# A two-layer graph network on one core: the first layer without the edges of nodes to themselves

## The chip, the core and the metric

The kernel runs on one core of a Trainium2 chip, in one launch. The metric is the time of the launch on the device in microseconds (us). The profile records one further execution of the same kernel, instruction by instruction.

## The reference, cut to what matters

There are 6250 nodes with 512 float32 features each, and 106250 directed edges: 50000 random ones, the same ones reversed, and one edge of each node to itself. They arrive sorted by destination (`dst`), and stably, so that a node's own edge is the last edge of its list (the own edges were appended last).

```python
def layer0(x, src, dst):                      # weights W_l, b_l, W_r
    agg = segment_sum((x @ W_l.T + b_l)[src], dst)     # sum over incoming edges
    deg = segment_sum(1, dst)
    return agg / max(deg, 1) + x @ W_r.T
x = layernorm(x + layer0(x, src, dst))

def layer1(h, src, dst):                      # summed by src: edges have to be sorted anew
    neigh = segment_sum((h @ W_neigh.T + b_neigh)[dst], src) / max(deg, 1)
    y = h + relu(h @ W_self.T + b_self + neigh)
    return layernorm(y) * ln_gamma + ln_beta
x = layernorm(x + layer1(x, src, dst))
```

## The kernel before, in words

**Tiles, runs and groups.** Both layers are done by `grouped` (L640 on). The sorted edges lie in tiles of 128 edges. For every tile, GpSimd (POOL) issues one indirect DMA that gathers the 128 source rows (2 KB each, 256 KB in all) into a row buffer; that is `fetched`, L633. There are 40 row buffers, used in turn. The edges are further cut into *runs* (the code calls them windows): stretches of edges whose nodes, at most H = 32, are summed together. In layer 0 a run is 3.5 tiles (CYCLE 2, 7: two runs every seven tiles), in layer 1, which leaves out the own edges, 3.25 tiles (CYCLE_L 4, 13). The nodes are divided into C = 4 parts, and one *group* takes one run of each part, so 4 x 32 rows of output. Layer 0 has 238 runs in 60 groups, layer 1 has 241 in 61.

**One group.** `match` (L180, `hot<-rel,cols`) builds on VectorE (DVE), for each tile of a run, a 128 x 32 matrix of zeros and ones: which edge belongs to which of the 32 nodes. `visits` (L740) multiplies that matrix with the gathered rows and adds up in PSUM (`agg`). The four runs of a group use four 32-column strips of TensorE (PE) side by side; I call the four matmuls that visit one tile of each run a *round*. A round is 8 records in the trace, since every float32 matmul has two. Runs of layer 0 touch 5 or 4 tiles in turn, because a run that ends within a tile shares that tile with the next one. `count` (L749) counts edges per node, `average` (L771) divides on ScalarE (ACT), `turn` transposes (L612, L614), `dense` projects by the two weight matrices (L620), `close` and `store` add bias and own rows, normalize (L554 to L570) and write the group's rows, 32 per part, to DRAM: `h_d` after layer 0, the output after layer 1. A group's own rows are loaded by SP (L727), 4 transfers per group, at a row number that SP reads from `lo_i`; the last groups, which would reach beyond the table, use an indirect DMA on POOL for it (L722), and for their stores as well (L793).

**Order of the work.** The order is written out by hand (`manual_schedule`), engine by engine. In the loop over groups g: `fetch(g+1)`, `match(g+1)`, the first two rounds of g, the transposed mean and the own projection of g-1, `store(g-2)`, `begin(g+1)` (own rows), the third round, the mean projection of g-1, own transpose, the other rounds, `count` and `average` of g, `close(g-1)`, then up to one step of the "other work" that uses PE, `shrink(g+1)` (L679), and up to five steps that use DVE alone. The other work in layer 0 is the sort of the edges by `src` for layer 1, a bitonic sort on DVE with transposes on PE (`Sorter.runs`). Layer 1 can start only when all of `h_d` is written.

**Start.** `first_rows` loads the indices of group 0, so that 19 gathers can start at once. `as_given` loads the edge lists (`given_k`, `next_i`, `given_v`), turns them by transposes into one column per tile (`node`, `idx`), `place` works out where runs begin and end (`lo`, `rel`) and whether the data fit this scheme (`flag`). If the flag is not zero, a slow fallback (`plain`, one tile after another) does the layer instead.

The lines that the prediction speaks of: L633 row gathers, L740 aggregation, L749 counting, L612 and L614 transposes, L620 projections, L180 the helper `both` (hot, sort steps, sums), L271 to L279 the first operations of the sort (`Sorter.load`), L722 and L793 indirect loads and stores of the last groups, L727 and L800 own rows and stores by SP.

Of the kernel before, what the change touches and what calls it, by code (L numbers as in the profile page):

```python
# [21 lines left out]
CYCLE = 2, 7  # L22
CYCLE_L = 4, 13
# [75 lines left out]
def kernel(  # L99
# [116 lines left out]
    class Sorter:  # L216


        def __init__(self, key, val, layer, pool, ps, loops, given=None):

            self.given = given
            self.pool, self.ps, self.layer, self.loops = pool, ps, layer, loops
            self.M = M if not loops else (E - N + P - 1) // P
            n, T = self.cycle = CYCLE_L if loops else CYCLE
            self.NW = (n * self.M + T - 1) // T

            Q = self.Q = (self.NW + C - 1) // C


            starts = [i * T * P // n - 1 for i in range(n + 1)]
            self.at = [v // P for v in starts[:n]]
            self.row_at = [v % P for v in starts[:n]]
            self.num = [b // P - a // P + 1 for a, b in zip(starts, starts[1:])]
            self.vis = max(self.num)
            self.key, self.val = key, val
            self.cur = None
            self.padded = const.tile([P, 1 + W], F32, name=f"node{layer}")
            self.node = self.padded[:, 1:]  # L240
            self.idx = const.tile([P, W], I32, name=f"idx{layer}")
            self.lo = const.tile([P, C * Q + 1], F32, name=f"lo{layer}")
            self.lo_i = const.tile([1, C * Q + 1], I32, name=f"lo_i{layer}")
            self.X = 1 if loops else 0
            self.rel = const.tile([P, Q, self.X + self.vis, C], F32, name=f"rel{layer}")
            self.flag = const.tile([1, 1], I32, name=f"flag{layer}")
            if loops:

                a = (E - N - CAP - 1) // P
                self.row = pool.tile([P, M - a], F32, name="row")  # L250
                nc.gpsimd.iota(self.row, pattern=[[P, M - a]], base=a * P - (E - N) + LOOP,
                               channel_multiplier=1, allow_small_or_imprecise_dtypes=True)
                self.more = const.tile([P, 1], F32, name="more")
                self.parts = 2 + (M - a - 1) // (W // CAP // 2 * 2)
# [10 lines left out]
        def load(self):  # L265
# [3 lines left out]
            if self.loops:  # L269
                v = self.pool.tile([P, W], I32, name="next_i")  # L270
# [76 lines left out]
        def as_given(self):  # L347


            full = M - 1  # L350
            ints = []
            for i, (v, fill, skip, eng) in enumerate((
                (self.key, NONE, 0, nc.sync), (self.key, NONE, 1, nc.scalar),
                (self.val, NONE, 0, nc.sync),
            )):
                t = self.pool.tile([P, blocks, P], I32, name=("given_k", "next_i", "given_v")[i])
                nc.vector.memset(t[:, full // P:, :], fill)
                a = full // P
                if a:
                    eng.dma_start(t[:, :a, :], v[skip:skip + a * P * P]  # L360
                                  .rearrange("(b p c) -> p b c", p=P, c=P))
                b = full % P
                if b:
                    eng.dma_start(t[:b, a, :], v[skip + a * P * P:skip + full * P]
                                  .rearrange("(p c) -> p c", c=P))
                r = E - full * P - skip
                if r:
                    eng.dma_start(t[b:b + 1, a, :r], v[skip + full * P:E].unsqueeze(0))
                ints.append(t)
            key, nxt, val = ints  # L370
            self.given = [t.rearrange("p b c -> p (b c)") for t in (key, val)]

            def columns(t, o):
                f = self.pool.tile([P, blocks, P], F32, name="srt", bufs=2)
                nc.vector.tensor_copy(f, t)
                p = self.ps.tile([P, 2 * D], F32, name="turn")
                for b in range(blocks):
                    nc.tensor.transpose(p[:, b * P:(b + 1) * P], f[:, b, :], ident)
                nc.scalar.copy(o[:, :D], p[:, :D])
                if o is self.idx:  # L380
                    nc.vector.tensor_scalar(o[:, D:W], p[:, D:W], float(N - 1), None, op0=ALU.min)
                else:
                    nc.vector.tensor_copy(o[:, D:W], p[:, D:W])

            columns(key, self.node)
            nc.vector.tensor_tensor(nxt, key, nxt, op=ALU.is_gt)
            worst = self.pool.tile([P, 1], F32, name="worst")
            nc.vector.tensor_reduce(worst, nxt.rearrange("p b c -> p (b c)"),
                                    axis=mybir.AxisListType.X, op=ALU.max)
            p = self.ps.tile([P, 2 * D], F32, name="turn")  # L390
            nc.tensor.matmul(p[:1, :1], worst, ones[:, :1], start=True, stop=True)
            odd = self.pool.tile([1, 2], F32, name="mixed")
            nc.vector.memset(odd, 0.0)
            nc.vector.tensor_copy(odd[:, :1], p[:1, :1])
            self.odd = odd
            return lambda: columns(val, self.idx)

        def first_rows(self):

            self.first = const.tile([P, C, self.vis], I32, name="first")  # L400
            for c in range(C):
                t = self.tiles(c * self.Q)
                k = max(0, -t.start)
                v = self.val[(t.start + k) * P:t.stop * P]
                nc.scalar.dma_start(self.first[:, c, k:len(t)], v.rearrange("(t p) -> p t", p=P))

        def unpack(self):
# [3 lines left out]
            n = self.pool.tile([P, W], I32, name="next_i")  # L411
# [69 lines left out]
        def place(self):  # L481
# [47 lines left out]
            if Q % n:  # L529
                nc.vector.memset(self.rel, -1.0)  # L530
# [11 lines left out]
            if self.loops:  # L542
                nc.vector.tensor_scalar(
                    self.rel[:, :, 0, :], lo[:, :C * Q].rearrange("p (c q) -> p q c", c=C), -1.0,
                    self.more, op0=ALU.mult, op1=ALU.add)
# [22 lines left out]
    def finish0(nr, po, own, some, work):  # L568
        po = po[:nr]
        nc.vector.scalar_tensor_tensor(po, biases["bl"][:nr], some[:nr], po,  # L570
                                       op0=ALU.mult, op1=ALU.add)
# [51 lines left out]
    def fetched(s, table, g, chunks, idx):  # L623


        for v in range(0 if g == 0 else 1, s.vis):
            for c in range(C):
                w = c * s.Q + g
                m = s.tiles(w)[v:v + 1]
                if w < s.NW and m and 0 <= m[0] < s.M:  # L630
# [5 lines left out]
                if w < s.NW and v == 1 and g:  # L636
                    t = s.tiles(w - 1)
                    chunks[w, 0] = chunks[w - 1, len(t) - 1]

    def grouped(s, table, w_n, w_s, layer, finish, dest, other, chunks, loads):  # L640
# [3 lines left out]
        with tc.tile_pool(name=f"g{layer}", bufs=2) as work, tc.tile_pool(  # L644
# [14 lines left out]
            def fetch(g):  # L659
                fetched(s, table, g, chunks, s.idx)  # L660
# [347 lines left out]
```

## Time and profile before

| what | us |
| --- | --- |
| median of 3 runs (2104.13 to 2106.35) | 2106.04 |
| the profiled execution | 2107.11 |
| its span, first to last instruction | 2105.3 |
| PE busy in the span | 1942.8 (92%) |
| POOL busy | 1558.7 (74%) |
| DVE busy | 1156.5 (55%) |
| first row gather issued | 5.94 |
| last row gather of layer 0, first of layer 1 | 1066.97, 1091.55 |
| last row gather of layer 1 | 2074.6 |

The profile's rows are to be read so. In the list in order of time, a row gives start, duration, engine, line, operation, output <- input, shape, how many were merged (`x8`), and in brackets how long the engine had been idle before and what ended that. In the list of groups, a row gives busy time and the mean in ns of one, then the idle time in front of them. A time of PE is not PE at its peak: a matmul that waits for its operands in the pipe counts as busy. `issue` stands for idle time in which the engine waited for nothing that the profile shows.

### The profile page before, as it was taken

Reading aid. Unit: us, or ns where it says so; the run is one execution under the profiler, and the core shown is the slowest. Engines: PE = TensorE matmul, PEld = TensorE weight load, DVE = VectorE, ACT = ScalarE, POOL = GpSimd, SP = SyncE. Lnnn points to the kernel's source line nnn. Section 1 sums busy time; section 2 is a strip of 40 time slices with the busy share of each in tenths; the row PEclk is TensorE's granted clock in tenths of the full one; section 3 lists DMA queues with packets and bytes.
Section 4 is the critical chain, followed back from the end, with each engine's and each line's share of the span. In section 5 each row is a group of like instructions: output and inputs, shape, how many; then the busy total and the mean of one; then the engine's idle time right before and its main releaser. Section 6 shows DMA issues by size and latency. Waiting matters only on the chain.

```text
span 2105.3 us, 26581 instructions
## 1 busy us (share of the span) xinstructions
PE 1942.8 (92%) x7561; PEld 658.8 (31%) x7561; DVE 1156.5 (55%) x2417; ACT 302.4 (14%) x631; POOL 1558.7 (74%) x1638
## 2 busy tenths in 40 slices
PE   4899999999999999999879999999999999999996
PEld 2333333333333333332322333333333333333332
DVE  4754455645555554342434556665666566655676
ACT  0111111111111111111101111111111111111111
POOL 7777777777777777777747777777777777777773
PEclk9999999999999999999989999999999999999998
DMA  9777778787888887878757788888878888887874
GB/s 265 223 231 234 239 235 239 238 240 237 244 253 251 252 247 239 238 235 241 230 149 220 240 245 244 241 240 243 247 241 240 244 244 244 240 240 244 245 240 122
DMA packets 184969, 495.94 MB, mean 236 GB/s; under 512 B 45911, under 2 KB 48401, under 8 KB 184806
## 3 DMA queue, kind: packets, MB, share of 16 engines
q0 software_dynamic: 130128, 426.15, 68.2%
q1 hardware_dynamic: 48308, 61.99, 9.4%
q10 hardware_dynamic: 6370, 5.94, 0.9%
q8 instruction: 64, 1.05, 0.2%
q14 instruction: 99, 0.81, 0.1%
HBM read 462.59 MB, written 31.65 MB: 235 GB/s over the span
## 4 chain that ended last, share of the span: by engine, by line
PE 55%; DMA 30%; issue 7%; POOL 6%; DVE 2%; POOLq 0%; ACT 0%; SPq 0%; ACTq 0%; DVEq 0%
PE po L620 29%; PE agg L740 20%; DMA rows<-h_d,idx 16%; DMA rows<-in_x_dram,idx 14%; POOL rows L633 6%; PE tp L612 4%; PE turn L308 0%; PE deg L749 0%; PE turn L469 0%; DMA first<-in_src_dram 0%; DMA own<-in_x_dram,slots 0%; DVE stats L554 0%; DVE po L570 0%; DVE v L180 0%; DVE srt L180 0%
## 5 line engine op out<-in xcount | busy, mean ns | idle before, releaser
L740 PE MATMUL agg<-rows,hot 128*32 128x512 f32 x4180 | 939.4, 614 | 105.4 <-DMA rows<-h_d,idx 41.0
L633 POOL DMA_INDIRECT rows<-in_x_dram,idx x815 | 786.7, 965 | 248.0 <-issue 116.8
L633 POOL DMA_INDIRECT rows<-h_d,idx x785 | 743.9, 948 | 241.6 <-issue 113.0
L620 PE MATMUL po<-wa,meanT 128*128 128x512 f32 (+1 forms) x968 | 447.5, 605 | 0.0
L620 PE MATMUL po<-wb,ownT 128*128 128x512 f32 (+1 forms) x968 | 436.3, 593 | 0.1
L740 PEld LDWEIGHTS agg<-rows,hot 128*32 128x32 f32 x4180 | 163.7, 109 | 667.0 <-DMA rows<-in_x_dram,idx 229.4
L603 DVE TENSOR_SCALAR inv<-deg 128x1 f32<-128x1 f32 (+1 forms) x60 | 9.5, 158 | 488.8 <-PE deg L749 488.8
L620 PEld LDWEIGHTS po<-wa,meanT 128*128 128x128 f32 (+1 forms) x968 | 173.0, 188 | 275.3 <-issue 254.4
L620 PEld LDWEIGHTS po<-wb,ownT 128*128 128x128 f32 (+1 forms) x968 | 173.8, 190 | 175.2 <-issue 174.9
L758 DVE TENSOR_SCALAR loops<-deg 128x1 f32<-128x1 f32 (+1 forms) x61 | 9.6, 158 | 341.1 <-PE deg L749 341.0
L180 DVE SCALAR_TENSOR_TENSOR srt<-srt 128x448 f32<-128x448 f32 (+3 forms) x313 | 180.4, 618 | 4.0
L614 ACT COPY ownT<-tp 128x512 f32<-128x512 f32 (+1 forms) x121 | 70.3, 581 | 758.9 <-PE tp L612 758.9
L679 DVE TENSOR_REDUCE hotb<-hot 128x128 bf16<-128x640 f32 x121 | 142.0, 1173 | 0.1
L771 ACT ACTIVATE mean<-agg,inv 128x512 f32<-128x512 f32 (+1 forms) x121 | 83.1, 687 | 386.7 <-DVE agg L767 177.3
L558 ACT ACTIVATE rstd<-mv,eps 128x1 f32<-128x1 f32 (+1 forms) x182 | 53.6, 295 | 415.5 <-DVE mv L556 410.6
L180 DVE SCALAR_TENSOR_TENSOR hot<-rel,cols 128x768 f32<-128x768 f32 (+1 forms) x121 | 102.3, 846 | 0.0
L614 ACT COPY meanT<-tp 128x512 f32<-128x512 f32 (+1 forms) x121 | 70.2, 580 | 204.1 <-PE tp L612 204.1
L612 PEld LDWEIGHTS tp<-ident,own 128*128 128x128 f32 (+1 forms) x484 | 60.5, 142 | 76.9 <-issue 74.2
L612 PEld LDWEIGHTS tp<-ident,mean 128*128 128x128 f32 (+1 forms) x484 | 51.1, 142 | 106.2 <-issue 53.5
L612 PE MATMUL tp<-ident,own 128*128 128x128 f32 (+1 forms) x484 | 73.1, 274 | 12.1 <-DMA own<-in_x_dram,slots 6.7
L612 PE MATMUL tp<-ident,mean 128*128 128x128 f32 (+1 forms) x484 | 79.6, 287 | 3.6 <-ACT mean L771 3.6
L564 DVE TENSOR_SCALAR po<-po,mv,rstd 128x512 f32<-128x512 f32 (+1 forms) x61 | 50.0, 819 | 2.2
(147 smaller groups left out, 879.0 us busy)
## 6 DMA issues: line engine op xcount, KB each, us to landing
own<-h_d SPq DMA_DIRECT2D x241, 64.0 KB
own<-in_x_dram SPq DMA_DIRECT2D x230, 64.0 KB
out_dram<-y SPq DMA_DIRECT2D x230, 64.0 KB
h_d<-y SPq DMA_DIRECT2D x227, 64.0 KB
rows<-in_x_dram,idx POOLq DMA_INDIRECT x815
rows<-h_d,idx POOLq DMA_INDIRECT x785
wa<-in_L_gnn_W_l_dram ACTq DMA_DIRECT2D x4, 256.0 KB
wb<-in_L_gnn_W_r_dram ACTq DMA_DIRECT2D x4, 256.0 KB
```

The lines of the kernel that those rows point to most:

```text
L180: nc.vector.scalar_tensor_tensor(o, a, 1.0, b, op0=ALU.mult, op1=op)
L558: nc.scalar.activation(root[:nr], mv[:nr, 1:2], AF.Sqrt, bias=eps[:nr])
L564: nc.vector.tensor_scalar(y, v, mv[:nr, 0:1], root[:nr], op0=ALU.subtract, op1=ALU.mult)
L603: nc.vector.tensor_scalar(inv[:nr], deg, 1.0, None, op0=ALU.max)
L612: nc.tensor.transpose(p[:, k, :nr], v[:nr, k * P:(k + 1) * P], ident[:nr, :nr])
L614: nc.scalar.copy(t[:, :, :nr], p[:, :, :nr])
L620: nc.tensor.matmul(po[:nr], aT[:, k, :nr], w[:, k, :], start=first and k == 0, stop=end and k == NK - 1)
L633: nc.gpsimd.indirect_dma_start(out=rows, out_offset=None, in_=table, in_offset=bass.IndirectOffsetOnAxis(ap=at, axis=0))
L679: nc.vector.tensor_reduce(hb[:, 0, :], hots[g][:, s.X * C:n * C].rearrange("p (v c) h -> p (c h) v", c=C), axis=mybir.AxisListType.X, op=A ...
L740: nc.tensor.matmul(agg[H * c:H * (c + 1), :], hot[:, C * (s.X + v) + c, :], chunks[w, v], start=v == have[0], stop=v == have[-1])
L758: nc.vector.tensor_scalar(st["loops"][:nr], deg[:nr, 1:2], 1.0, None, op0=ALU.add)
L771: nc.scalar.mul(st["mean"][:nr], st["agg"][:nr], st["inv"][:nr])
```

## The change

Layer 0 gets its own class, `Given`, beside `Sorter`, which from now on serves layer 1 alone.

- Runs of layer 0 are now 3 whole tiles long (`TILES = 3`), plus the last tile of the run before: 4 rounds per group throughout. There are 66 runs per part, 264 in all, so 66 groups. In each part the first 4 runs (`WIDE`) hold 384 edges as given. The other 62 are cut from the list every 404 edges (`RAW`); their own edges are taken out, and what remains (384 if 20 were taken, less if more were) fits the same 3 tiles. The sum for such runs gets its own rows added (`average`), and 1 is added to the count (`count`).
- Taking them out happens on the chip. 124 partitions hold two runs each; every edge knows how many places it has to move (0 to 31, from the count of nodes before it), and five rounds of "shift those with bit i by 2^i" pack them (`narrow`). These operations are the first pieces of the other work in the loop, ahead of the sort: all of the DVE ones stand behind `shrink(1)` of group 0, the transposes (`turned`) and the copies into `idx`, `node` and `rel` (`placed`) in group 1.
- Because the packed indices are not there at the start, the indices of groups 0 to 3 are loaded separately: `first` for group 0 and `lines`, turned by a transpose into `second`, for groups 1 to 3. The gathers of group 1 are issued ahead of the flag as well (`EARLY = 2`).
- Where runs begin is no longer found by matmuls but loaded from `dst` (`li`, `back`), so that SP's row numbers come from DRAM directly. The test of the data (`flag`) checks the numbers of nodes per run among others.
- The 40 row buffers become a ring of fixed tiles. `finish0` adds the bias without the factor `some`.

The built program issues 795 row gathers in layer 0 where 834 stood, and 47 transfers on SP and ACT ahead of the weights of layer 0 where 13 stood; on POOL, one of the two own-row gathers of the last groups now stands behind the last row gather.

The diff, cut to its core:

```diff
-CYCLE = 2, 7
-CYCLE_L = 4, 13
+CYCLE = 4, 13
+TILES = 3
+WIDE = 4
+RAW = 404
+FEWEST = RAW - TILES * P
+MOST = 31
+EARLY = 2
 ROWS = 40
...
+    class Given(Sorter):
+        loops = False
+        def shape(self):
+            self.X, self.vis, self.M = 0, TILES + 1, M
+            self.wide = WIDE * TILES * P
+            part = (E + C - 1) // C
+            self.pairs = (part - self.wide + 2 * RAW - 1) // (2 * RAW)
+            self.Q = WIDE + 2 * self.pairs
+            self.NW = C * self.Q
...
+        def rows(self, w, v):
+            c, g = divmod(w, self.Q)
+            m = TILES * g + v
+            if g == 0:
+                return self.first[:, c, v:v + 1]
+            if g < WIDE:
+                return self.second[:, c * self.near_cols + m:c * self.near_cols + m + 1]
+            return self.idx[:, c * self.cols + m:c * self.cols + m + 1]
...
+        def ask(self, spare):
...
+            for t, k, d, eng in ((self.li, 2, -1, nc.scalar), (self.back, 1, -1 - BACK, nc.sync)):
+                for c in range(C):
+                    for g, step, num in ((0, TILES * P, WIDE), (WIDE, RAW, self.Q - WIDE)):
...
+                        eng.dma_start(
+                            t[:, w:w + num - skip, :],
+                            bass.AP(tensor=dst.tensor, offset=dst.offset + at,
+                                    ap=[[E, 1], [step, num - skip], [1, k]]))
...
+            for t, v, fill in ((self.wk, dst, N), (self.wv, src, 0)):
...
+                    nc.sync.dma_start(
+                        t[c * pairs:c * pairs + k, :],
+                        bass.AP(tensor=v.tensor, offset=v.offset + c * L + self.wide,
+                                ap=[[2 * RAW, k], [1, 2 * RAW + 1]]))
...
+        def turn_lines(self):
+            n = 2 * C * self.near_cols
+            f = self.fresh()
+            nc.vector.tensor_copy(f[:n, :P], self.lines[:n])
+            p = self.ps.tile([P, 2 * D], F32, name="turn")
+            nc.tensor.transpose(p[:, :n], f[:n, :P], ident[:n, :n])
...
+        def narrow(self):
...
+            def taken():
+                two(a, w, val, ALU.is_equal)
+                two(b, w, nxt, ALU.not_equal)
+                two(a, a, b, ALU.bitwise_and)
+            def moves():
+                by_bits(a, a, -1, ALU.add)
+                two(pairs(b), pairs(w), pairs(w)[:, :, :1].to_broadcast([top, 2, RAW]),
+                    ALU.subtract)
+                by_bits(b, b, 2 * BITS, ALU.logical_shift_left)
+            def packed():
+                nc.vector.tensor_scalar(w, w, NONE, BITS, op0=ALU.bitwise_xor,
+                                        op1=ALU.logical_shift_left)
+                two(w, w, val, ALU.bitwise_or)
+                two(w, w, b, ALU.bitwise_or)
+                two(w, w, a, ALU.bitwise_and)
+            def move(i):
+                d = 1 << i
+                nc.vector.tensor_scalar(b, w, 31 - 2 * BITS - i, 31, op0=ALU.logical_shift_left,
+                                        op1=ALU.arith_shift_right)
+                two(b, b, w, ALU.bitwise_and)
+                two(w, w, b, ALU.bitwise_xor)
+                to = pairs(w)[:, :, :RAW - d]
+                two(to, to, pairs(b)[:, :, d:], ALU.bitwise_or)
...
+            def turned():
+                p = self.ps.tile([P, 2 * D], F32, name="turn")
+                f = pairs(self.wk[:top, :n].bitcast(F32))
+                for j in range(2 * TILES):
+                    i, m = divmod(j, TILES)
+                    nc.tensor.transpose(p[:, j * P:j * P + top], f[:, i, m * P:(m + 1) * P],
+                                        ident[:top, :top])
+                self.x = self.fresh()
+                nc.scalar.copy(chunks(self.x), chunks(p))
+            def placed():
...
+                nc.vector.tensor_scalar(u, x, BITS, NONE, op0=ALU.logical_shift_right,
+                                        op1=ALU.bitwise_and)
...
+                for c in range(C):
+                    nc.vector.tensor_scalar(to[0][:, c], of[0][:, c], NONE, None,
+                                            op0=ALU.bitwise_and)
+                    nc.vector.tensor_scalar(to[1][:, c], of[1][:, c], -1.0, float(NONE),
+                                            op0=ALU.mult, op1=ALU.add)
+                self.nodes_less_first(self.node, m, WIDE, self.Q)
+            runs = [taken, moves, packed, *(lambda i=i: move(i) for i in range(5)), end]
+            for i in range(0, len(runs), 2):
+                yield False, lambda i=i: [r() for r in runs[i:i + 2]]
+            yield True, turned
+            yield False, placed
...
                 if not s.loops:
-                    st["inv"], st["some"] = inverse(deg[:nr, :1], nr, work)
+                    st["inv"] = work.tile([P, 1], F32, name="inv")
+                    nc.vector.tensor_scalar(st["inv"][:nr], deg[:nr, :1], 1.0, None,
+                                            op0=ALU.max if g < WIDE else ALU.add)
+                    nc.vector.reciprocal(st["inv"][:nr], st["inv"][:nr])
                     return
...
+                elif g >= WIDE:
+                    both(st["agg"][:nr], st["agg"][:nr], st["own"][:nr], ALU.add)
                 st["mean"] = work.tile([P, D], F32, name="mean")
...
-    s0.first_rows()
+    s0.ask((s1.padded.bitcast(I32), s1.idx))
+    s1.given, s1.next = s0.given[::-1], s0.next
     first = {}
-    fetched(s0, x, 0, first, s0.first)
-    rest = s0.as_given()
+    fetched(s0, x, 0, first)
+    s0.turn_lines()
+    for g in range(1, EARLY):
+        fetched(s0, x, g, first)
...
+    def meanwhile():
+        yield from s0.narrow()
+        yield from sort_and_place(s1)
...
-        grouped(s0, x, *w0, 0, finish0, h_d, sort_and_place(s1), first, loads)
+        grouped(s0, x, *w0, 0, finish0, h_d, meanwhile(), first, loads)
```

In the original, `a` and `b` are scratch tiles of 124 x 808 int32, `w` and `val` the destinations and sources of two runs per partition, `nxt` the destinations one place further on, `two` a tensor_tensor and `by_bits` a tensor_scalar on DVE.

## The prediction

> **What bounds the kernel now.** I read the engine totals first, then one steady stretch of POOL and PE in order of time, then the longest waits, then the start and the seam between the layers. The totals and the group of row gathers:
>
> ```profile
> PE 1942.8 (92%) x7561; PEld 658.8 (31%) x7561; DVE 1156.5 (55%) x2417; ACT 302.4 (14%) x631; POOL 1558.7 (74%) x1638
> ...
> L633 POOL DMA_INDIRECT rows<-in_x_dram,idx x815 | 786.7, 965 | 248.0 <-issue 116.8
> L633 POOL DMA_INDIRECT rows<-h_d,idx x785 | 743.9, 948 | 241.6 <-issue 113.0
> ```
>
> PE looks like the bound at 92%. The order of time contradicts it, POOL first, then PE in the same stretch:
>
> ```profile
> 412.01 0.95 POOL L633 DMA_INDIRECT rows<-in_x_dram,idx  x1 [0.30 <-PE agg L740]
> 413.26 0.95 POOL L633 DMA_INDIRECT rows<-in_x_dram,idx  x1 [0.30 <-DMA rows<-in_x_dram,idx]
> 414.51 0.95 POOL L633 DMA_INDIRECT rows<-in_x_dram,idx  x1 [0.30 <-PE agg L740]
> 415.76 0.95 POOL L633 DMA_INDIRECT rows<-in_x_dram,idx  x1 [0.30 <-issue]
> ```
>
> ```profile
> 414.16 0.66 PE L612 MATMUL tp<-ident,mean 128*128 128x128 f32 x4
> 414.65 3.60 PE L620 MATMUL po<-wb,ownT 128*128 128x512 f32 x8
> 418.18 1.07 PE L740 MATMUL agg<-rows,hot 128*32 128x512 f32 x8
> 419.18 3.70 PE L620 MATMUL po<-wa,meanT 128*128 128x512 f32 x8
> 422.71 0.60 PE L612 MATMUL tp<-ident,own 128*128 128x128 f32 x4
> 423.25 1.90 PE L740 MATMUL agg<-rows,hot 128*32 128x512 f32 x10
> 426.28 2.74 PE L740 MATMUL agg<-rows,hot 128*32 128x512 f32 x6 [1.14 <-DMA rows<-in_x_dram,idx]
> 428.96 0.18 PE L749 MATMUL deg<-ones_b,hotb 128*128 128x1 bf16 x1
> 429.07 4.29 PE L740 MATMUL agg<-rows,hot 128*32 128x512 f32 x16
> ```
>
> POOL starts a gather every 1.25 us (0.95 busy, 0.30 between), whatever is named as releaser, and never waits longer. PE's aggregation stretches instead: 16 records take 4.29 us where rows are late, 8 take 1.07 where they are there. So the gathers' beat sets the pace. It adds up: layer 0 has 19 + 815 row gathers and 2 of own rows, from 5.94 to 1066.97 us; 835 intervals of 1.25 are 1043.8, the rest 17.3. Layer 1 has 785, 1091.55 to 2074.6: 784 x 1.25 = 980.0, rest 3. The seam takes 24.6, the end 30.7.
>
> The Trainium skill's page "Perfetto Trace Analysis", section Identifying the Most-Contended Engine, holds occupancy to be a fair measure for GpSimd and a bad one for matmuls. The second half agrees with the 4.29 against 1.07 above; by the first half POOL at 74% would have a quarter to spare, and dropping gathers would pay only 0.95 us each (40 x 0.95 = 38 us). The rows show the 0.30 to recur like work, so the beat decides.
>
> **What the change removes.** The program as built has 795 row gathers in layer 0 (264 runs of 3 tiles, and 3 more) for 834. With one own-row gather instead of two ahead of the last row gather (the other comes behind it), intervals go from 835 to 795: **-40 x 1.25 = -50.0 us**, if the beat stays the limit. Layer 1 keeps its 785.
>
> **Does PE stay below the beat?** A new group has 12 gathers: 15.0 us. PE per group from the rows above: projections 3.60 + 3.70, transposes 0.66 + 0.60, counting 0.18, and 4 rounds of aggregation (for 5 or 4) at 1.07: 13.0 us. Groups of 12 gathers exist already: every second one in layer 0, counted from one L749 row to the next, takes about 15.2 us. The 6 added groups (66 for 60) bring PE 6 x 8.74 = 52.4 us less 6 rounds x 1.07, +46 us, inside the 2 us per group that PE has free. If that cover goes, the +46 shows: rival 1. The added sum of own rows to agg (L767's kind in layer 1: 0.76) lies between count and mean; layer 1 has the same chain and holds the beat. DVE is busy 55%, 9.6 us of the mean 17.5 per group, sort steps included, and so has room in 15. SP issues 8 transfers per group at 0.70 to 0.87 us: up to 7 of 15. The bytes per group fall slower than its time: 14 x 256 KB in 15 us is 245 GB/s, and the profile's slices of layer 1 show 240 to 247.
>
> **The start: a wait is added.** The first 51 gathers (groups 0 to 3) need no packed indices; the 52nd needs the first copy of the packing. By the beat it is due at 5.9 + 51 x 1.25 + 0.4 (flag) = 70 us. What leads to its index:
>
> 1. Loads. 47 transfers on SP and ACT, where 13 stood, and in the program as built each waits for the one eight before it. A small one needs 4.4 us here (the index list `first`, 1.27 to 5.66). So four per queue in 4.4 us, 1.1 us apart: the 18 that SP issues from 4.7 us to the last `back` end at about 22, landed by 25. Then some 8 us of short DVE rows (0.15 to 0.6 each; nbad's reduction 0.64): the first `hot` at about 33, for 28.41.
> 2. Group 0's own rows and count follow as before (inv at 43.38), so at 48. Behind it on DVE: shrink, then the packing, all 31 operations in one go.
> 3. The packing. Its operations are new; the nearest rows are these:
>
> ```profile
> 51.22 1.08 DVE L271 TENSOR_TENSOR next_i<-given_v,given_k 128x896 int32<-128x896 int32 x1
> 52.34 0.63 DVE L272 TENSOR_SCALAR next_i<-next_i 128x896 int32<-128x896 int32 x1
> 53.00 1.09 DVE L273 TENSOR_TENSOR next_i<-next_i,given_k 128x896 int32<-128x896 int32 x1
> ```
>
> Start to start 1.12 and 0.66; at 808 columns 1.01 and 0.60. 22 of the first kind and 9 of the second: 27.6 us, from 49 to 76.5.
>
> 4. Queued in front of the copy: group 2's hot (0.7), group 1's inv (0.35), closing of group 0 (0.69 + 0.69 + 0.72 + 0.18), rstd and a copy of 744 columns on ACT (0.3 + 0.8), one more int operation (0.6): the index at about **82 us, a stall of 12**.
>
> Bounds. Nothing lost in step 1 (start as before) gives 7; all 31 operations at 0.60 as well gives none. Loads at twice the spacing (+10 us), or own rows held up by the weights that now load later, give 22 to 25. I keep 12, the sum of the rows, and 0 to 25 for the range. Of before's 17.3 us of excess, 4.1 fall in its first 100 us and are replaced: the start costs 12 + 1 - 4.1 = **+9**. The delay of PE in those 30 us is hidden: 40 row buffers hold three groups.
>
> **DVE against POOL.** While DVE runs back to back on two SBUF operands, gathers lengthen:
>
> ```profile
> 50.71 1.01 POOL L633 DMA_INDIRECT rows<-in_x_dram,idx  x1 [0.30 <-issue]
> 52.03 1.09 POOL L633 DMA_INDIRECT rows<-in_x_dram,idx  x1 [0.30 <-DMA rows<-in_x_dram,idx]
> 53.42 1.49 POOL L633 DMA_INDIRECT rows<-in_x_dram,idx  x1 [0.30 <-DMA rows<-in_x_dram,idx]
> 55.21 1.36 POOL L633 DMA_INDIRECT rows<-in_x_dram,idx  x1 [0.30 <-issue]
> ```
>
> About 1.2 us lost in 6, so 5 in the 27.6 of the packing, less than the 12 that POOL waits there anyway: cost 0, or 5 if the stall is gone. The sort's own excess (13.2 us from 100 us on) is the same work and stays.
>
> The Trainium skill's page "SBUF — State Buffer", section SBUF: two separate sides, speaks against the change here: the port pair of DVE and GpSimd is an exclusive lock, and the loser blocks fully. By it the packing would hold POOL for its whole length, the 52nd gather would be asked for at about 97 us, and the sum would be 15 us higher, near 2079. The rows show a gather finishing beside such operations in 1.0 to 1.5 us.
>
> **The seam and the end.** The last group is full (12 gathers, before 9), so PE is not behind at the end, but its own rows come by an indirect gather queued behind the last row gather. From the last gather I get 7 us to count (before 7.8), then the same chain: 23.5 for 24.6, **-1**, bounds -4 to +3. Layer 1 and the end: 0.
>
> **Sum.** -50.0 + 9 - 1 = -42, from the profiled execution's 2107.1 (span 2105.3 and 1.8 around it): 2065. The median of the runs lies 1.1 lower: **2064 us**.
>
> **Rivals.**
> 1. *PE becomes the pace* (slower). It decides when a group costs PE over 15.0 us, 2 above the 13.0 counted. For it: 92%, and po and agg hold half of the chain that ended last. Against it: the 12-gather groups at 15.2. The gathers dropped then pay nothing and the 46 us show: 2107 + 46 = 2153. Chance 0.06.
> 2. *The indices come far later*, 25 us or so of stall at the 52nd gather, by slow loads or by DVE held up: 2064 + 13 = 2077, with the row-buffer backlog up to 2085. For it: 47 queued loads, and the weights behind them; against it: 10 us of slack after step 1. Chance 0.17.
> 3. *The beat stretches* in layer 0, since 12 gathers now share 15 us with as much sort work and own traffic as 14 did: 1.27 for 1.25 is 795 x 0.02 = +16: 2080. Layer 1 at 1.25 with 16.1 us groups speaks against it. Chance 0.08.
> 4. *The start is free*: no stall: 2052. Chance 0.06.
> 5. *It doesn't do what it says*: the flag sends layer 0 down the fallback, 831 steps each behind three dependent DMAs of some 4 us: over 10 ms. From the reference's inputs each run of 404 holds 20 to 28 own edges, within the 20 to 31 allowed, but at its edge. Chance 0.01.
>
> Forecast 0.62. The range 2050 to 2085 takes in cases 2, 3 and 4 and leaves 1, 5 and misses out. About 0.2% is what a measurement can tell here. Faster 0.92 (forecast, 2, 3, 4, less a little for stalls above 40 us), same 0.01, slower 0.07.
>
> **What would show it.** Gathers from x at 1.25 us, 795 of them, layer 0's last near 1025 us; one gap on POOL near 70 us, released by DVE's copy, of 0 to 25 us; layer 1's first gather 23 to 25 us after layer 0's last; layer 1 unchanged. Wrong: PE gapless with gathers waiting for free rows (rival 1), gathers over 1.27 us in the middle (3), or a gap before 70 us (flag or `second` late).

## The result, and the profile after

The changed kernel takes 2113.75 us (median of 7 runs, 2108.86 to 2117.61) against 2106.04 for the kernel before in the same comparison (7 runs, 2101.59 to 2106.84): a ratio of 1.0041, with a 95% interval of 1.0027 to 1.0054. It is slower by 0.4%, where 2064 was forecast. Its profiled execution took 2112.57, with a span of 2110.7. In two later comparisons, that of e8 and e9 and that of e12, every kernel, the one before too (2503.47 and 2541.3), took 19% to 21% longer, so that of these only the ratios, the order of events in the first 100 us and the DRAIN at the end are read.

The page after, engine totals, the slices of DMA, and the group of row gathers:

```profile
PE 1899.0 (90%) x7674; PEld 664.8 (31%) x7674; DVE 1247.7 (59%) x2518; ACT 313.9 (15%) x654; POOL 1520.1 (72%) x1598
...
GB/s 248 111 131 245 247 249 239 239 244 240 250 258 254 262 259 244 240 245 245 240 152 220 243 246 242 240 242 246 242 240 242 247 242 240 242 246 243 241 241 100
...
L870 POOL DMA_INDIRECT rows<-in_x_dram,idx x744 | 717.7, 965 | 279.1 <-issue 95.1
L870 POOL DMA_INDIRECT rows<-h_d,idx x785 | 743.5, 947 | 242.0 <-issue 108.2
```

The gathers are fewer, as counted (744, and 51 with their indices in `first` and `second`), and cost 965 ns each as before. What is new stands in the second and third slice (53 us each): 111 and 131 GB/s, where every other slice has 239 or more, apart from the seam (152 and 220) and the end (100). POOL in order of time shows why:

```profile
69.05 0.95 POOL L870 DMA_INDIRECT rows<-in_x_dram,second  x1 [0.30 <-DMA rows<-in_x_dram,second]
70.30 0.95 POOL L870 DMA_INDIRECT rows<-in_x_dram,second  x1 [0.30 <-issue]
123.94 0.95 POOL L870 DMA_INDIRECT rows<-in_x_dram,idx  x1 [52.70 <-DVE idx L770]
125.20 0.94 POOL L870 DMA_INDIRECT rows<-in_x_dram,idx  x1 [0.30 <-DVE node L772]
```

Apart from single gathers of 1.0 to 1.9 us and 1.5 us of waiting for the flag, the beat of 1.25 us holds up to the 51st gather, and it is there again from the 52nd on. The 52nd was due at 71.6 and came at 123.94: one stall of 52.4 us, at the place where 12 were forecast. DVE tells what it waited for:

```profile
42.93 0.68 DVE L186 SCALAR_TENSOR_TENSOR hot<-rel,cols 128x512 f32<-128x512 f32 x1
89.02 0.16 DVE L991 TENSOR_SCALAR inv<-deg 128x1 f32<-128x1 f32 x1 [45.41 <-PE deg L986]
89.21 0.17 DVE L993 RECIPROCAL inv<-inv 128x1 f32<-128x1 f32 x1
89.29 1.06 DVE L916 TENSOR_REDUCE hotb<-hot 128x128 bf16<-128x512 f32 x1
90.27 1.00 DVE L714 TENSOR_TENSOR next_i<-node,idx 124x808 int32<-124x808 int32 x1
...
117.51 0.58 DVE L745 TENSOR_SCALAR node<-node 124x808 int32<-124x808 int32 x1
...
122.72 0.47 DVE L770 TENSOR_SCALAR idx<-srt 128x186 int32<-128x186 int32 x1
```

DVE stood idle for 45 us ahead of `inv` of group 0, and the packing stands behind it in DVE's queue. In the kernel before, that wait was 12.26:

```profile
43.38 0.16 DVE L603 TENSOR_SCALAR inv<-deg 128x1 f32<-128x1 f32 x1 [12.26 <-PE deg L749]
```

The count `deg` (PE) is queued behind the transpose of the own rows, which waited for their DMA until 85.89. And SP's queue in the changed kernel:

```profile
19.24 7.47 SPq L589 DMA_DIRECT2D back<-in_dst_dram  x8
28.51 13.92 SPq L601 DMA_DIRECT2D node<-in_dst_dram  x4
42.48 0.25 SPq L605 DMA_DIRECT2D node<-in_dst_dram  x1
52.09 12.63 SPq L601 DMA_DIRECT2D idx<-in_src_dram  x4
64.77 1.23 SPq L605 DMA_DIRECT2D idx<-in_src_dram  x1
66.10 0.65 SPq L1190 DMA_DIRECT2D h_d<-tail  x1
68.82 22.55 SPq L964 DMA_DIRECT2D own<-in_x_dram  x12
```

The ten loads that bring `dst` and `src` for the packing (`node<-in_dst`, `idx<-in_src`: the tiles of layer 1 serve as their buffers) keep SP from 28.5 to 66. Before, SP issued the first own rows at 30.94; now at 68.82, though the flag was there at 39.63. The kernel before:

```profile
30.94 10.38 SPq L727 DMA_DIRECT2D own<-in_x_dram  x12
```

How slow these loads are shows in two stretches of the changed kernel (the engines' busy time, then the granted clock, the DMA engines' busy share, GB/s; in the second, the DMA engines are little more than half busy):

```profile
28.00:52.00 24.00, 6.44 (x28) 2.01 (x28) 10.02 (x36) 1.28 (x1) 17.33 (x19) 0.93 0.87 302
52.00:82.00 30.00, 0.00 (x0) 0.00 (x0) 0.00 (x0) 0.00 (x0) 14.65 (x18) 0.50 0.58 175
```

And from 72 to 82 us, when the gathers have stopped (in the second half of the line only these loads are left):

```profile
GB/s 259 259 210 275 210 177 128 46 29 13 29 29 29 29 13 29 29 29 16 26 29 29 29 16 26 26 26 26 26 26 26 26 26 26 26 26 26 26 18 14
```

26 GB/s is one packet of 3236 B after another, 0.13 us each. The trace has one packet per row: 246 of 3236 B and two of 2888, from 31.8 to 81.6 us. One alone was under way for 24.3 us, more than one for 2.2, and none for the rest. Six of the eight big loads have 31 rows: 186 rows at 0.13 us make up the 24.3. The 2.2 are two short bursts, at 43.5 and 65.5, in which up to 11 are under way at once: the two loads of 30 rows. So a load of 31 rows goes row by row. Alone, at the end (from 78 us on), a row starts every 0.13 us; beside other transfers it was every 0.28 to 0.37 for the most part. The Trainium skill's page "DMA: Bandwidth & Descriptors", section "Why a DMA increments its semaphore by 16 and not by 1", has the rule: a transfer is spread over the largest number of DMA engines up to 16 that divides its row count, so 30 rows over 15 and 31 over one. The packets agree (11 at once, and one at a time).

Theory A is then: the 31-row loads cost the 40 us. Rivals: B, the bytes (loads, weights and gathers fill the memory system together); C, the packing's own cost; D, only the order on SP, the loads being quick by themselves.

### The profile page after: what moved, and what is told of

It is laid out like the page before. It is cut to its first block, busy times and chain, and to the rows that moved or that the text cites. A ratio compares the mean times of both kernels' runs of the same rounds, so it can differ in the third digit from the quotient of the medians.

```text
span 2110.7 us, 27121 instructions
## 1 busy us (share of the span) xinstructions
PE 1899.0 (90%) x7674; PEld 664.8 (31%) x7674; DVE 1247.7 (59%) x2518; ACT 313.9 (15%) x654; POOL 1520.1 (72%) x1598
## 5 line engine op out<-in xcount | busy, mean ns | idle before, releaser
L977 PE MATMUL agg<-rows,hot 128*32 128x512 f32 x4154 | 848.0, 613 | 89.2 <-DMA rows<-h_d,idx 37.0
L870 POOL DMA_INDIRECT rows<-in_x_dram,idx x744 | 717.7, 965 | 279.1 <-issue 95.1
L858 PE MATMUL po<-wa,meanT 128*128 128x512 f32 (+1 forms) x1016 | 469.7, 605 | 0.0
L858 PE MATMUL po<-wb,ownT 128*128 128x512 f32 (+1 forms) x1016 | 458.6, 594 | 0.0
L977 PEld LDWEIGHTS agg<-rows,hot 128*32 128x32 f32 x4154 | 147.8, 109 | 564.4 <-DMA rows<-h_d,idx 224.5
L858 PEld LDWEIGHTS po<-wa,meanT 128*128 128x128 f32 (+1 forms) x1016 | 182.1, 189 | 288.6 <-issue 267.6
L991 DVE TENSOR_SCALAR inv<-deg 128x1 f32<-128x1 f32 x66 | 10.4, 158 | 388.3 <-PE deg L986 388.3
L186 DVE SCALAR_TENSOR_TENSOR srt<-srt 128x448 f32<-128x448 f32 (+4 forms) x320 | 184.6, 618 | 4.0
L916 DVE TENSOR_REDUCE hotb<-hot 128x128 bf16<-128x512 f32 (+1 forms) x127 | 141.6, 1115 | 0.1
L186 DVE SCALAR_TENSOR_TENSOR hot<-rel,cols 128x512 f32<-128x512 f32 (+1 forms) x127 | 102.2, 805 | 0.0
```

The source lines that it names most:

```text
L186: nc.vector.scalar_tensor_tensor(o, a, 1.0, b, op0=ALU.mult, op1=op)
L858: nc.tensor.matmul(po[:nr], aT[:, k, :nr], w[:, k, :], start=first and k == 0, stop=end and k == NK - 1)
L870: nc.gpsimd.indirect_dma_start(out=rows, out_offset=None, in_=table, in_offset=bass.IndirectOffsetOnAxis(ap=s.rows(w, v), axis=0))
L916: nc.vector.tensor_reduce(hb[:, 0, :], hots[g][:, s.X * C:n * C].rearrange("p (v c) h -> p (c h) v", c=C), axis=mybir.AxisListType.X, op=A ...
L977: nc.tensor.matmul(agg[H * c:H * (c + 1), :], hot[:, C * (s.X + v) + c, :], chunks[w, v], start=v == have[0], stop=v == have[-1])
L991: nc.vector.tensor_scalar(st["inv"][:nr], deg[:nr, :1], 1.0, None, op0=ALU.max if g < WIDE else ALU.add)
```

## The experiments

Times of each are compared with the kernel before on the same chip (2104.84 to 2106.91 where nothing else is said).

### e1: the loads cut in two

```diff
-                    nc.sync.dma_start(t[c * pairs:c * pairs + k, :], ...)
+                    h = (k + 1) // 2
+                    for a, b in ((0, h), (h, k)):
+                        nc.sync.dma_start(t[c * pairs + a:c * pairs + b, :], ...)
```

> Each of the eight big loads of dst and src for the packing (31 rows of 3236 B, or 30) is cut into two of 16 and 15 rows (15 and 15); nothing else changes. Theory A, the row count: a transfer of 31 rows is carried one row after another, so the 248 rows of 0.13 us take from 31.8 to 81.6 us, and SP's own rows wait behind them; pieces of 15 or 16 rows are carried side by side. Then own rows of group 0 land near 47 instead of 85.9, inv at 50 instead of 89, the 52nd gather at 84 (gap on POOL 14 instead of 52.7), and the time is 39 us below 2113.75: 2070 to 2080. Rival B, bytes: the loads, the weights and the gathers share a full memory system, and the pieces need as long as the whole: gap 50 or more, time 2110 to 2118. Rival C, the packing itself (DVE and POOL in each other's way): gap unchanged too.

Measured: 2089.78 us, 0.9915 of before (0.9898 to 0.9931), 24 below the changed kernel. The same bytes landed by 51.0 instead of 81.6, own rows reached PE at 58.46, `inv` came at 61.59, the gap on POOL was 25.2. Theory A holds; B and C by themselves fall. But the gap is not the 14 expected. The stretch from 28 to 52 us of this kernel shows what is left:

```profile
28.00:52.00 24.00, 7.36 (x28) 2.08 (x28) 9.80 (x36) 1.28 (x1) 18.47 (x20) 0.95 1.04 333
```

The DMA engines are now full (1.04, for 0.87). Loads, weights and gathers together need until 51, and own rows come behind. That is what rival B says of the remaining time; no run here takes the weights away to show it.

### e2: the packing ahead of the count; e3: both

```diff
+                    if g == 0 and not s.loops:
+                        more(5, False)
+                        more(1, True)
+                        more(1, False)
                     count(g)
```

> The loads as in the changed kernel; the packing, its transposes and the copies to idx, node and rel stand ahead of count(0) on DVE, PE and ACT, so that they need no own rows. Theory A: the packing then waits for the loads themselves (last packet 81.6 us): from 82 to 110, the 52nd gather near 113 (gap 42 instead of 52.7), time near 2103. If only the own rows' lateness counted and the loads were there in time: packing from 44 to 72, gather at 75, gap 4, time near 2066.

> Both edits of the two runs before. Theory A: packing from about 47 to 75, the 52nd gather at 78, gap 8, and 6 less than the run with the cut loads alone: 2064 to 2074. Rival B: as the run with the packing first, near 2103.

Measured, e2: 2111.17 (1.0019; 1.0010 to 1.0029), gap 41.6, the 52nd gather at 112.05, as theory A has it; the time is 8 above its estimate, since PE is later too and a further gap of 3.9 us follows. DVE of e2 shows that the packing itself waits for its data now:

```profile
39.42 0.68 DVE L186 SCALAR_TENSOR_TENSOR hot<-rel,cols 128x512 f32<-128x512 f32 x1
80.13 1.00 DVE L714 TENSOR_TENSOR next_i<-node,idx 124x808 int32<-124x808 int32 x1 [40.03 <-DMA idx<-in_src_dram]
```

So the own rows were never the root, only the first to show it. e3: 2080.05 (0.9869; 0.9853 to 0.9886), above the 2064 to 2074 expected. The packing waited for loads until 51.33, and now it runs while POOL gathers (lines of e1 and e3 stand 3 lower than those of the changed kernel):

```profile
56.93 0.94 POOL L873 DMA_INDIRECT rows<-in_x_dram,second  x1 [0.30 <-DMA rows<-in_x_dram,second]
58.18 1.74 POOL L873 DMA_INDIRECT rows<-in_x_dram,second  x1 [0.30 <-issue]
60.22 1.35 POOL L873 DMA_INDIRECT rows<-in_x_dram,second  x1 [0.30 <-DMA rows<-in_x_dram,second]
61.87 1.77 POOL L873 DMA_INDIRECT rows<-in_x_dram,second  x1 [0.30 <-issue]
63.95 1.34 POOL L873 DMA_INDIRECT rows<-in_x_dram,second  x1 [0.31 <-issue]
```

Gathers of 1.3 and 1.8 us for 0.95: beside DVE's packing POOL loses some 0.6 us per gather. DVE in the same stretch shows how much each loses:

```profile
58.10 1.00 DVE L717 TENSOR_TENSOR node<-node,sign 124x808 int32<-124x808 int32 x1
60.17 0.58 DVE L740 TENSOR_SCALAR sign<-node 124x808 int32<-124x808 int32 x1
61.82 2.03 DVE L717 TENSOR_TENSOR node<-node,sign 124x808 int32<-124x808 int32 x2
63.88 0.58 DVE L740 TENSOR_SCALAR sign<-node 124x808 int32<-124x808 int32 x1
```

Each of the four long gathers starts within 0.1 us of the start of a DVE operation and ends 0.82 or 0.83 us after that operation's end: 59.92 for 59.10, 61.57 for 60.75, 63.64 for 62.82 (the first of the two), 65.29 for 64.46. The next operation, which starts 0.03 us later, costs it nothing more. The short waits belong to operations with one operand in SBUF, the long ones to those with two.

### e4: the uncut loads on ACT's queue

```diff
-                    nc.sync.dma_start(
+                    nc.scalar.dma_start(
                         t[c * pairs:c * pairs + k, :], ...)
```

> The eight big loads uncut, but issued by ACT ahead of the weights instead of by SP; nothing else changes. Theory A (rows one after another, in whatever queue): own rows of group 0 land near 45, but the loads still end at 65 to 82 us and the packing waits for them: the 52nd gather at 98 to 115 (gap 27 to 44), time 2088 to 2105; the weights land later than now. Rival D, only SP's order (the loads are quick by themselves, own rows merely stand behind waits in SP's queue): packing from 49 to 77, gather at 82, gap 12, time near 2073.

Measured: 2103.99 (0.9980; 0.9970 to 0.9990), the 52nd gather at 111.02. Both lie where theory A put them, but not by its path. The loads ended at 58.6, not at 65 to 82, and the packing, which began at 77.25, did not wait for them: it waited for `inv` (76.02). `back`, on SP and 1 KB in all, was read 16 us later than in the changed kernel (48.58, not 32.57), the flag came as late (55.61), and own rows, issued at 60.44, reached PE at 72.88, not near 45. POOL waited 17.6 us for the flag.

```profile
48.58 0.28 DVE L649 CAST srt<-back 1x264 f32<-1x264 int32 x1 [20.13 <-DMA back<-in_dst_dram]
```

What the run does show: on ACT's queue the rows go one at a time too (one alone under way for 23.8 us), so the loads are not quick by themselves, and D falls. And another queue doesn't spare the small loads: from 39 to 47.5 us the trace has the 4-byte packets of `back` and the rows of ACT's loads in turn, nearly always one of each. That fits the same DMA engine for both, but no view here names the engine.

### e5, e8, e10: towards a version without the stall

e5 issues the cut loads (`dst` by SP, `src` by ACT) ahead of everything but the index lists and packs before `place`:

```diff
-EARLY = 2
+EARLY = 3
...
+    drain(s0.narrow())
     s0.place()
...
-        yield from s0.narrow()
```

e8 is e3 with `src`'s loads on ACT ahead of the weights; e10 is e8 with `EARLY = 3`:

```diff
-            for t, v, fill in ((self.wk, dst, N), (self.wv, src, 0)):
+            for t, v, fill, eng in ((self.wk, dst, N, nc.sync), (self.wv, src, 0, nc.scalar)):
```

> A version meant to be best. The big loads, cut in two as in the first run, are issued right behind the index lists: dst's by SP, src's by ACT, ahead of the lists for the sort and of li and back. The packing, its transposes and copies stand ahead of place on DVE, PE and ACT (with another scratch tile), and three groups instead of two are gathered ahead of the flag. Theory A (what costs is when the packed index is there): loads land near 22, packing 22 to 52, idx near 55, no gap at the 52nd gather; in its place place comes later, flag near 62 for the 40th gather due at about 61, a gap of 0 to 5, and gathers beside the packing of 1.8 to 2.1 us instead of 1.25 (as seen with both edits: 7 to 9 us lost). Time 2062 to 2072. Rival E: the gain is given back, since group 0's hot and all of PE start at 65 instead of 40 and the row buffers fill: gaps of 10 and more behind the 40th gather, time 2076 or more, as with both edits.

> As the run with both edits (loads cut in two, packing ahead of count(0)), and src's big loads issued by ACT ahead of the weights while SP issues dst's. With both edits alone the loads landed at 50.2 us and the packing ran from 51.3 to 79, though DVE was free from 41.5. Theory A: the loads land near 38 to 40, the packing runs from 41.5 to 70, idx near 73; the 52nd gather is due at about 75 (gathers beside the packing are slower), so the gap of 8.3 us goes, and part of the one of 5.6 us at 100: time 8 to 12 us below 2080, 2066 to 2073. Rival H: li and back land later because the queues are fuller, the flag comes after 42, and the gap turns up ahead of it: 2076 or more.

> As e8_queues, and three groups instead of two are gathered ahead of the flag (39 gathers, which fit the 40 row buffers). In e8_queues the loads no longer held up the packing (46.1 to 74), but POOL waited 6 us at 38 us for the flag: rival H took back what the loads gave. Theory A with that term: the wait at 38 us goes, the 52nd gather is due at about 77 beside the packing's end, no gap over 3 us: 5 to 6 us below the run with both edits, 0.983 to 0.986 of the kernel before (2070 to 2076). Rival: nothing gained (0.987), because the 52nd gather waits for the index, 77 us, in any case.

Measured, e5: 2079.45 (0.9875; 0.9859 to 0.9892). Its packing ran from 21 to 49 and the 52nd gather waited for nothing, but the time is that of rival E: the flag came at 68.9, `agg` of group 0 at 72.7, and behind the 39th gather two came 8.1 and 4.1 us apart. e8: 0.9925 (0.9905 to 0.9945) of its own before. The loads did what was asked (packing from 46.09, no wait), but POOL waited 5.1 us for the flag, from 39.1 to 44.2. That looks like rival H and isn't shown to be: `back` was read at 30.55, earlier than in the changed kernel, and it is DVE's chain to the flag that stood idle for 1.8 and 2.6 us, for nothing that the profile shows. Idle times of that kind (1.9 to 2.6 us) stand in e9 and e12 as well, and in no other run. In e10, with the same loads as e8, the flag came at 36.69; so what the third group ahead of the flag is worth by itself is open. With both waits gone, e10: **2069.85 us, 0.9832 (0.9819 to 0.9846)**, better than both kernels. POOL at the place of the stall:

```profile
72.15 0.95 POOL L873 DMA_INDIRECT rows<-in_x_dram,second  x1 [0.30 <-PE agg L980]
73.40 0.95 POOL L873 DMA_INDIRECT rows<-in_x_dram,second  x1 [0.30 <-DVE idx L773]
74.65 2.61 POOL L873 DMA_INDIRECT rows<-in_x_dram,second  x1 [0.30 <-issue]
77.56 0.95 POOL L873 DMA_INDIRECT rows<-in_x_dram,second  x1 [0.30 <-issue]
```

No gap is left. The 52nd gather comes at 78.82, 11 us behind an undisturbed beat (3.74 + 51 x 1.25 = 67.5), because gathers beside DVE's operations take longer (10.7 us of it).

### e11: e10 without the shifts

```diff
-            runs = [taken, moves, packed, *(lambda i=i: move(i) for i in range(5)), end]
+            runs = [taken, moves, packed, end]
```

> As e10_three, without the five rounds of shifts (20 of the packing's 31 DVE operations, 18.5 us of 27.7): own edges leave holes and the last 20 edges of each narrow run are dropped, so the first layer's sums leave edges out; the gathers are as many. It prices the packing that remains in e10_three. If DVE's operations cost POOL nothing: the same time within 2 us. If gathers beside them take 1.8 to 2.1 us instead of 1.25, as in the two runs with the packing first: 20 operations in 18.5 us cost POOL some 6 us, 5 to 8 us below e10_three.

Measured: 2064.39 (0.9805; 0.9791 to 0.9818), 5.5 below e10. That is the price of 20 integer operations of DVE (18.5 us) to a POOL that has work: they cost POOL 30% of their own time.

### e6, e7, e9, e12: the end

The ledger (below) has 4.7 us at the end that no step foresaw. POOL ends with three DRAINs; the long one, called the last DRAIN here, is 4.95 us longer, which covers it. This is the row of the kernel before and of the changed one (shortest, median, longest in ns):

```profile
L1004 POOLq DRAIN  x3: 45/113/4564, 2099.9 to 2105.1; - x3
```

```profile
L1252 POOLq DRAIN  x3: 45/113/9510, 2100.4 to 2110.4; - x3
```

e6 and e12 add 40 and 24 gathers of single words in POOL's long wait, e9 adds 8 (to e8) at the last group of layer 0, in the same form; e7 is the kernel before, unaltered.

```diff
+        if not s.loops and g == WIDE:
+            for i in range(40):
+                nc.gpsimd.indirect_dma_start(
+                    out=spare[:, i:i + 1], out_offset=None, in_=dst.unsqueeze(1),
+                    in_offset=bass.IndirectOffsetOnAxis(ap=s.second[:, 1:2], axis=0))
```

> The changed kernel with 40 further gathers of 128 single words (from dst, into columns that nothing reads) on POOL ahead of the 52nd gather, inside the 52.7 us in which POOL waits there: 1627 indirect DMAs, as many as before. At the end POOL's last DRAIN took 4.56 us before and 9.51 in the changed kernel and in all four runs so far (1587 indirect DMAs each), though the last packet of the last store ends 2.4 us after its issue in all. Theory F, the number of indirect DMAs sets it: DRAIN 4.56 again, from the last gather to the end 31 to 32 us instead of 35.4. Rival G, something else in the program: 9.51 again. The 52nd gather comes at 120 to 128, as in the changed kernel.

> The kernel before, unaltered, profiled once more. If the last DRAIN is set by the program: 4.56 us again, the end 30.7 us from the last gather. If it varies from run to run: some other number, and the 4.9 us between the ends of the two kernels are chance.

> As e8_queues, with 8 further gathers of 128 single words (nothing reads them) on POOL at the last group of layer 0, where POOL waits 9.4 us between its own-row gather and the first store: 1595 indirect DMAs. With 1627 the last DRAIN took 4.5 us (three profiles), with 1587 it took 9.51 (seven). If the DRAIN goes by the number within some power of two up to 32 (1595 leaves 11 and 27 as 1627 does): 4.5, and the time is 5 us below e8_queues. If it falls evenly with the number: 8.5, 1 us below. If neither: 9.5 and no gain.

> The changed kernel with 24 further gathers of single words in POOL's long wait: 1611 indirect DMAs. The last DRAIN so far: 9.51 us at 1587, 10.16 at 1595, 4.5 at 1627. From 1587 to 1595 that is 0.08 us per DMA. If the DRAIN rises evenly and falls back at some number: 11.4 where the fall lies above 1611, or 3.2 (4.5 less 16 x 0.08) where it lies below. Any other value: no such law.

| indirect DMAs | last DRAIN, us |
| --- | --- |
| 1587 (the changed kernel, e1 to e5, e8, e10, e11) | 9.51 in each |
| 1595 (e9) | 10.16 |
| 1611 (e12) | 3.95 |
| 1627 (before; e7; e6) | 4.56; 4.49; 4.52 |

e6 took 2118.35 in its one run, since the added gathers outlasted the wait (the 52nd gather came at 132.9, not at 120 to 128), but its DRAIN is that of the kernel before, as theory F has it; G falls. In e7 the DRAIN is the same again, with 32.0 us from the last gather to the end instead of 30.7. e9 gained nothing: 0.9952 (0.9937 to 0.9968) against e8's 0.9925; its eight gathers made the seam 10 us longer. e12 took 2552.97 against 2541.3, one run each; its 3.95 is neither of the two values that an even rise with one fall would give (11.4 or 3.2). So the number of indirect DMAs decides, but by a law that four numbers don't give: 0.65 us more from 1587 to 1595, 6.2 less by 1611, 0.6 more by 1627. Why was not tried.

## Why the prediction was wrong, step by step

The ledger of the profiled executions, in us of the span (2105.3 to 2110.7):

| step | predicted | measured |
| --- | --- | --- |
| 40 intervals of 1.25 less | -50 | -50 |
| first gather at 3.74 instead of 5.94 | not seen | -2.2 |
| layer 0's time beyond the beat, 17.3 before | +9 | +53.5 (70.8) |
| seam (24.3 for 24.6) | -1 | -0.3 |
| layer 1 | 0 | -0.3 |
| the end | 0 | +4.7 |
| sum | -42 | +5.4 |

- **The gathers pay 1.25 each: right.** The -50 of the table is counted, 40 intervals of 1.25. That they are worth it shows outside the start, where layer 0 keeps its beat: 11.0 us beyond it from 150 us on, 11.8 in the kernel before. The beat does not stretch (rival 3).
- **PE stays below the beat: right**, and cheaper than counted. After the stall, six groups in a row come 12.0 to 12.4 us apart (13.0 predicted), later ones 15. Rival 1 falls.
- **Start, step 1 (loads of the index lists): too early by 8.** The last `back` was read at 32.57 instead of 25, the first `hot` came at 41.24 instead of 33. Some of it is in the sum itself: four transfers per queue in 4.4 us put the 18th at 22.3 and its landing at 26.7.
- **Start, step 2: the step that failed.** "Group 0's own rows and count follow as before (inv at 43.38), so at 48": `inv` came at 89.02. The 47 transfers were counted and the last `back` put at 25, but the ten that stand behind it on SP, ahead of the own rows, were given no time, neither in front of the own rows nor as the packing's input. Their row count, which the code shows, set their pace: their rows went one at a time from 31.8 to 81.6, and cut in two (e1) they had landed by 51.0. With 89 in place of 48 the prediction's own sum gives 123 for the 52nd gather; it came at 123.94.
- **Steps 3 and 4: right.** Packing 27.6 predicted, 90.27 to 118.1 = 27.8 measured; from there to the gather 5.5 and 5.8.
- **DVE against POOL: right in sign, hidden here as forecast**, since POOL stood still. Where it is not hidden it costs more than the 5 that were priced: 5.5 for two thirds of the packing (e10 against e11), and 8.4 for all of it by the durations of the gathers of e10, each less 0.95. The prediction took the Trainium skill's page "SBUF — State Buffer", section SBUF: two separate sides, to hold POOL for the whole packing. The page says for the whole instruction, and the rows of e3 agree: a gather waits for the end of the one operation that it meets.
- **The end: not 0 but +4.7**, from the number of indirect DMAs.
- Rival 2 ("slow loads") was the case that came true, at 52 us of stall instead of 25. It thought of many small loads and of the weights, not of the rows of the big ones, and the 10 us of slack that it held against itself left these out.

e10 gives the check from the other side: with the stall taken out, the same 40 intervals bring 39.4 us of span (-50 - 2.2 + 6.1 beyond the beat + 0.5 seam - 0.4 layer 1 + 6.6 end), near the forecast -42. That it comes so near is partly luck: 6.6 at the end and -2.2 at the first gather were not in the forecast, and the 6.1 are longer gathers, where it had a stall.

## What to carry to other kernels

Give every transfer that a change adds a time of its own, from its shape as well as its bytes, and follow the queue past it to whatever stands behind; a count of transfers is not a time. When a wait goes up a chain (POOL for DVE, DVE for PE, PE for own rows, own rows for SP), undo the links one at a time: here the loads at its end also fed the packing directly, and moving the packing alone brought 2111 for 2114. A row count such as 31 is easy to avoid (16 + 15), and to overlook it cost 24 us here.

## What the runs showed of the hardware

- A load of 31 rows of 3236 B goes one row of 0.13 us after another, at 26 GB/s when it is alone; the same bytes in pieces of 16 and 15 rows end 31 us earlier, at a DMA share of 1.04 (333 GB/s in all).
- Such a load holds up small transfers of the other queue too: `back` was there 16 us later when ACT instead of SP issued the large loads, and its 4-byte packets took turns with their rows.
- A gather that starts beside an int32 operation of the packing on DVE ends 0.82 us after that operation: 1.34 us behind one of 0.58 us with one SBUF operand, 1.74 to 1.77 behind one of 1.00 with two, for 0.95 alone; 18.5 us of such operations cost POOL 5.5.
- POOL's last DRAIN depends on the number of indirect DMAs in the program (9.51 us at 1587, 4.5 at 1627), to 0.07 us from run to run; with 40 gathers fewer it was 5 us longer here, with 16 fewer (1611) 0.6 shorter.
